# Expert choice: wider table rows from kept buffers, scales copied by ScalarE, and a new order of rows, statistics and choosing passes

## The chip, the core and the metric

The kernel runs on one core of a Trainium2 chip. Its engines work side by side, each through its own queue of instructions in order: TensorE (PE in the profile; PEld is its loading of weights), VectorE (DVE), ScalarE (ACT), GpSimd (POOL), and SyncE (SP), which here only issues DMA transfers. They wait for each other by semaphores. The metric is the device time of one execution in microseconds, the median of several runs.

## What is computed

The program is a four-layer network on an image tensor of 4 images, 128 channels and 64x64 positions. Each layer adds a convolution-like block and then a block on the tokens (the 4096 positions of an image, 128 values each) to the running tensor. The change concerns the token block of layers 1 and 2, a mixture of 64 experts in which each expert chooses its 8 best tokens of each image. Cut to what matters:

```python
def expert_choice(x, gate_w, gate_b, weight1, weight2):      # x: normed tokens, (4, 4096, 128)
    logits = einsum('bsd,ed->bse', x, gate_w) + gate_b       # 64 experts
    probs = softmax(logits, axis=1)                          # over the tokens of an image
    topv, topi = top_k over tokens, K = 8                    # per image and expert
    gathered = x[b, topi]                                    # (4, 8, 64, 128)
    pooled = einsum('bked,bke->bed', gathered, topv)
    h = gelu(einsum('ebd,edh->ebh', [pooled, 1], weight1))   # 512 hidden values
    out = einsum('ebh,eho->ebo', [h, 1], weight2)
    outputs[b, topi] += out * topv
    return outputs

t = t + expert_choice(layernorm(t), ...)                     # in layers 1 and 2
```

## The kernel before

The running tensor `xs` stays on chip for the whole program, channels on the 128 partitions and the 4096 tokens of each image along the free dimension. `net.chunk(b, c)` is a block of 512 tokens (`CH`) of image `b`; an image has 8 of them (`NCH`). The phases of the network run one after the other; `expert_choice(net, layer)` (L911) is called once in layer 1, after the deformable convolution, and once in layer 2, after a 3x3 convolution. Inside it all engines execute instructions in the order in which the Python code issues them (`tc.manual_schedule`), so the loops at the end of a stage are a schedule written out by hand. A tile pool hands out buffers; `bufs=5` means that the sixth tile of this tag waits until the first is no longer used. `bank("a", ...)` and `bank("b", ...)` are PSUM banks, three of each.

The work is done for pairs of images: pair 0 is images 0 and 1, pair 1 is images 2 and 3. A pair fills the partitions as 2 images x 64 experts, so the logits of a pair, `chosen[p]`, are 128x4096.

**Stage 1, choosing** (pool `moe_a`). At the start SyncE loads the gate, the biases and the weights of the first 3 of 16 groups of experts (L985, L987).
- `stat(p, j)` (L1008, L1010): TensorE centres a block, ScalarE squares it; every fourth block `variances` (L1018) sums squares over channels by four small products. 16 blocks for a pair.
- `scales(p)` and `inverted(p)` (L1031, L1035): square root on ScalarE and reciprocal on VectorE give 1/standard deviation of each token, as rows; `turn_scales(p)` (L1041, L1043) transposes them, so that a token's scale stands in its partition.
- `logits(p, c)`: TensorE spreads the scales over the partitions with a column of the identity, one product for each image (L1054), and multiplies the gate with the tokens (L1062). ScalarE copies the spread scales out of PSUM (L1066), VectorE multiplies (L1067), ScalarE adds the bias (L1068).
- `largest(p)`: VectorE finds the 8 largest of 4096 (L1087), their places (L1090), and the row numbers; two passes over 128x4096.
- `exponentials(p, neg)`: ScalarE takes the exponential of all logits, with their sum (L1101), and of the 8 (L1103). One buffer, `exps`, serves both pairs.
- `rows(b, c)`: the tokens are written to a table in DRAM, one row for each token. TensorE transposes four times 128 tokens (L1076), ScalarE copies them to `moe_xt` (L1078), GpSimd puts the token's scale behind the 128 values (L1079), and SyncE writes the block of 512 rows (L1081). A row has `ROW` = 129 numbers, 516 bytes. 8 blocks for an image, 32 in a call.
- `ask(p, j)` (L1108): GpSimd gathers, for each expert and image of the pair, the row of its j-th choice, by an indirect DMA.
- `pool(p)`: VectorE makes diagonal matrices of share x scale (L1122), TensorE sums the gathered rows with them (L1130), ScalarE copies (L1132), TensorE centres (L1134), VectorE puts the result into `pooled` (L1135).
- `mark(p)` (L972) and `choose(p)` (L977): VectorE overwrites the 8 largest logits with a mark, and then turns the whole 128x4096 into exponentials where the mark is and zero elsewhere. They are needed only in stage 3.

The order of stage 1 before: two statistics, the gate product (L1142) and the transposes of the first bias (L1147), the other statistics of pair 0, five of pair 1, the logits of pair 0, `largest(0)`, the rest of pair 1's statistics, the exponentials of pair 0, then the rows of images 0 and 1 with the logits of pair 1 between, then the rows of images 2 and 3 with the last logits, `largest(1)`, `mark(0)`, `choose(0)` and the gathers of pair 0; the exponentials and gathers of pair 1; `pool(0)`, `pool(1)`.

**Stage 2, experts** (pools `moe_b`, `moe_w_b`). 16 groups of 4 experts. `first` (L1201) and `second` (L1227) are the two products, `turn` (L1213, L1215, L1220) transposes, adds the bias and applies the gelu, `hand` (L1246) collects the results. Each group's weights are 2 MB. Five buffers hold them: three taken at the start of the call, two in memory that stage 1 used, so that SyncE's fourth load waits for the end of stage 1. VectorE also does `mark(1)` in turn 4 and `choose(1)` in turn 7 of the loop.

**Stage 3** (L1278, L1282): one product per block brings the experts' results back to the chosen tokens, and VectorE adds it to `xs`.

Of the kernel before, what the change touches and what calls it, by code (L numbers as in the profile page):

```python
# [910 lines left out]
def expert_choice(net, layer):  # L911
# [19 lines left out]
    PAIRS = B // 2  # L931
    K, ROW = 8, P + 1
    EARLY, LATE = 3, 2
    GONE = -3.0e38
    w1, w2 = ins[f"L{layer}_ffn_weight1"], ins[f"L{layer}_ffn_weight2"]
    with ExitStack() as ctx:
# [30 lines left out]

        tops = {}

        def mark(p):  # L970
# [20 lines left out]
        with (  # L991
# [56 lines left out]
            def logits(p, c):  # L1048
                pb, pl = bank("b", "rb"), bank("a", "pl")
                q = c % 4  # L1050
                rows = slice(32 * q, 32 * q + 32)
                for i in range(2):
                    own = 32 * q + 2 * i + c // 4
                    nc.tensor.matmul(  # L1054
                        pb[i * E : (i + 1) * E],
                        net.ident[rows, own : own + 1].to_broadcast([32, E]),
                        rstds[p][rows],
                        start=True,
                        stop=True,
                    )  # L1060
                for i in range(2):
                    nc.tensor.matmul(  # L1062
                        pl[i * E : (i + 1) * E], cgate, net.chunk(2 * p + i, c), start=True, stop=True
                    )
                lg = chosen[p][:, c * CH : (c + 1) * CH]
                nc.scalar.copy(lg, pb)  # L1066
                nc.vector.tensor_mul(lg, lg, pl)  # L1067
                nc.scalar.activation(lg, lg, AF.Identity, bias=gbias)  # L1068

            def rows(b, c):  # L1070

                p, i = divmod(b, 2)
                pt = bank("b", "pt")
                for t in range(4):
                    tok = slice((4 * c + t) * P, (4 * c + t + 1) * P)
                    nc.tensor.transpose(pt[:, t * P : (t + 1) * P], net.xs[:, b, tok], net.ident)  # L1076
                xt = sb.tile([P, 4, ROW], F32, name="moe_xt", tag="moe_xt", bufs=5)
                nc.scalar.copy(xt[:, :, 0:P], pt.rearrange("p (t d) -> p t d", d=P))  # L1078
                nc.gpsimd.tensor_copy(xt[:, :, P], turned[p][:, i, c, :])  # L1079
                first = i * N + c * CH  # L1080
                nc.sync.dma_start(tables[p][first : first + CH, :].rearrange("(t p) r -> p t r", p=P), xt)  # L1081
# [3 lines left out]
            def largest(p):  # L1085
# [9 lines left out]
                nc.vector.tensor_copy(places[p], row)  # L1095
                neg = sb.tile([P, 1], F32, name="moe_neg", tag="moe_neg")
                nc.vector.tensor_scalar_mul(neg, top[:, 0:1], -1.0)
                return neg

            def exponentials(p, neg):  # L1100
                nc.scalar.activation(exps, chosen[p], AF.Exp, bias=neg, accum_out=totals[p])  # L1101
                shares[p] = sb.tile([P, K], F32, name="moe_share", tag="moe_share")
                nc.scalar.activation(shares[p], tops[p], AF.Exp, bias=neg)  # L1103

# [33 lines left out]

            for j in range(2):
                stat(0, j)  # L1140
            pg = bank("b", "pg")
            nc.tensor.matmul(pg[:, 0:E], net.cent, gate, start=True, stop=True)  # L1142
            nc.vector.tensor_copy(cgate, pg[:, 0:E])

            pg = bank("b", "pb").rearrange("p (i c) -> p i c", i=NH)
            for i in range(NH):
                nc.tensor.transpose(pg[:, i, 0:E], b1[:, i:HID:NH], net.ident[0:E, 0:E])  # L1147
            nc.vector.tensor_copy(b1t, pg[:, :, 0:E])
            for j in range(2, 2 * NCH):
                stat(0, j)  # L1150
            scales(0)
            inverted(0)
            for j in range(5):
                stat(1, j)
            turn_scales(0)
            for c in range(NCH):
                logits(0, c)
            neg = largest(0)
            for j in range(5, 2 * NCH):
                stat(1, j)  # L1160
            scales(1)
            exponentials(0, neg)
            inverted(1)
            for n in range(2 * NCH):
                rows(*divmod(n, NCH))
                if n == 5:
                    turn_scales(1)
                if n > 5 and n % 2 == 0:
                    logits(1, n // 2 - 3)
            for n in range(2 * NCH):  # L1170
                rows(2 + n // NCH, n % NCH)
                if n < 6 and n % 2 == 0:
                    logits(1, 5 + n // 2)
                if n == 5:
                    neg = largest(1)
                    mark(0)
                    choose(0)
                if 5 < n < 6 + K:
                    ask(0, n - 6)
            exponentials(1, neg)  # L1180
            for j in range(K):
                ask(1, j)
            pool(0)
            pool(1)

        ob = ctx.enter_context(tc.tile_pool(name="moe_out", bufs=1))
        ots = [ob.tile([P, D], F32, name=f"moe_ot{i}") for i in range(PAIRS)]
        with (
# [66 lines left out]
            for g in range(GROUPS + 3):  # L1255
# [6 lines left out]
                if 0 <= g - 3:  # L1262
                    hand(g - 3, outs.pop(g - 3))
                if g == 4:
                    mark(1)
                if g == 7:
                    choose(1)
# [705 lines left out]
```

## Time and profile before

| what | us |
|---|---|
| median of 3 runs | 8528.07 (8521.14 to 8533.63) |
| the profiled execution, its own time | 8199.67 |
| span of the profiled execution, first to last instruction | 8197.9 |
| layer 1, stage 1 (from 2795.9) | 141.3 |
| layer 1, stage 2 (from 2937.2) | 80.1 |
| layer 1, stage 3 (from 3017.3) | 20.4 |
| layer 2, stage 1 (from 3356.9) | 137.0 |
| layer 2, stage 2 (from 3493.9) | 81.6 |
| layer 2, stage 3 (from 3575.5) | 20.5 |

Busy shares of the whole span on the profile's page: TensorE 92%, VectorE 67%, GpSimd 65%, ScalarE 46%. In stage 1 of layer 1 (141.3 us) the windows view gives busy times of 109.3 (TensorE), 53.0 (VectorE), 68.4 (ScalarE) and 26.5 (GpSimd), and a mean DMA share of 0.56.

How to read the lines below. A line of a timeline gives start and length in us, the engine, the line of the kernel, the operation, the tile written and the tiles read, the shape and the number of instructions merged; the bracket is the idle time of the engine before it and what ended it. "SPq" is SyncE issuing a DMA. A window line gives the length and the busy times of the engines in it with their instruction counts. The mean clock that TensorE was granted was 0.965 of full.

### The profile page before, as it was taken

What the parts mean: (1) busy time and instruction counts of PE and PEld (TensorE: products, weight loads), DVE (VectorE), ACT (ScalarE), POOL (GpSimd) and SP (SyncE); (2) the same over time, 40 slices, a digit from 0 to 9 for tenths busy, and PEclk for the clock granted to TensorE, in tenths of its full rate; (3) what the DMA queues carried; (4) which work ended last, traced back from release to release, by engine and by line L of the source; (5) the groups of instructions that cost most, each with busy time, mean ns of one, the idle gap of its engine ahead of it and who ended that gap; (6) DMA issues with size and microseconds to landing.
All of it is one profiled execution on the core that took longest, in us unless ns stands there. A gap on an engine that the chain in (4) does not pass through costs nothing.

```text
span 8197.9 us, 144876 instructions
## 1 busy us (share of the span) xinstructions
PE 7560.4 (92%) x59022; PEld 3232.8 (39%) x59022; DVE 5530.6 (67%) x8689; ACT 3768.7 (46%) x7100; POOL 5299.3 (65%) x3019
## 2 busy tenths in 40 slices
PE   8999986777777779879999999999999999999899
PEld 2222243555555434333444344443444434444333
DVE  6888856888888642247776667766677677677155
ACT  4444433444444420313555555555555555555521
POOL 5888904777777410104888788887788777888700
PEclk9999998999999989988999999999999999999999
DMA  6434206877877570232554445554545444455400
GB/s 183 93 77 95 50 2 158 249 220 237 241 217 209 161 211 0 46 146 57 108 110 105 103 105 104 110 106 99 107 101 111 105 101 106 106 105 110 98 22 24
DMA packets 333940, 963.78 MB, mean 118 GB/s; under 512 B 43412, under 2 KB 148948, under 8 KB 275412
## 3 DMA queue, kind: packets, MB, share of 16 engines
q0 software_dynamic: 143872, 673.30, 34.9%
q1 hardware_dynamic: 189396, 281.18, 12.7%
q8 instruction: 464, 7.60, 0.4%
q14 instruction: 208, 1.70, 0.1%
HBM read 468.89 MB, written 82.78 MB: 67 GB/s over the span
## 4 chain that ended last, share of the span: by engine, by line
PE 53%; DVE 2%; issue 1%; DMA 1%; ACT 0%; POOL 0%; SPq 0%; POOLq 0%; DVEq 0%; ACTq 0%
PE att_pv L1576 15%; PE att_sc L1663 13%; PE att_mx L1520 11%; PE att_sc L1564 5%; PE top_po L1876 3%; PE top_pw L1852 1%; DVE att_most L1531 1%; DMA moe_w<-in_L_ffn_weight 1%; PE att_sc L1493 0%; PE att_sc L1607 0%; PE att_sc L1624 0%; PE top_po L1874 0%; PE att_mx L1418 0%; PE att_sc L1454 0%; PE att_sc L1520 0%
## 5 line engine op out<-in xcount | busy, mean ns | idle before, releaser
L1595 POOL TENSOR_TENSOR att_acc<-att_acc,att_ex 128x2048 f32<-128x2048 f32 x640 | 2902.3, 4535 | 637.5 <-ACT att_ex L1664 618.1
L1531 DVE TENSOR_REDUCE att_most<-att_mx 128x2 f32<-128x1024 f32 x2016 | 2461.9, 1222 | 1071.3 <-PE att_mx L1520 992.7
L1664 ACT ACTIVATE att_ex<-att_sc 128x512 f32<-128x512 f32 x4096 | 2223.7, 594 | 1771.1 <-PE att_sc L1663 1488.0
L1663 PE MATMUL att_sc<-att_q,att_k 32*128 32x512 f32 x8192 | 2455.6, 606 | 0.0
L1520 PE MATMUL att_mx<-att_k,att_q 32*128 32x512 f32 x8064 | 2292.1, 647 | 12.9 <-DVE att_parts L1543 10.8
L1564 PE MATMUL att_sc<-att_rows,att_ones_b 32*128 32x256 bf16 (+1 forms) x6144 | 1502.5, 306 | 4.7 <-ACT att_ex L1664 4.7
L816 POOL DMA_INDIRECT dcn_g<-dcn_table,dcn_idx x1152 | 1100.8, 956 | 433.4 <-DMA dcn_g<-dcn_table,dcn_idx 122.5
L1576 PE MATMUL att_pv<-att_ex,att_vals 128*32 128x256 f32 x16384 | 1309.8, 391 | 0.0
L1520 PEld LDWEIGHTS att_mx<-att_k,att_q 32*128 32x128 f32 x8064 | 610.9, 185 | 867.1 <-issue 707.2
L409 POOL TENSOR_TENSOR inv_prod<-inv_seen,inv_prod 128x512 f32<-128x512 f32 (+1 forms) x672 | 837.4, 1273 | 95.4 <-ACT inv_prod L408 95.4
L411 DVE SCALAR_TENSOR_TENSOR inv_prod<-inv_pk,bspan,inv_seen 128x512 f32<-128x512 f32 (+1 forms) x1120 | 774.5, 743 | 141.4 <-PE inv_pk L398 141.1
L1576 PEld LDWEIGHTS att_pv<-att_ex,att_vals 128*32 128x32 f32 x16384 | 322.5, 108 | 1318.9 <-issue 1300.8
L1663 PEld LDWEIGHTS att_sc<-att_q,att_k 32*128 32x128 f32 x8192 | 818.3, 183 | 11.0 <-issue 8.3
L830 ACT ACTIVATE dcn_one<-dcn_g,dcn_w 128x128 f32<-128x128 f32 x1152 | 458.0, 401 | 790.9 <-DMA dcn_g<-dcn_table,dcn_idx 785.6
L857 PE MATMUL dcn_pt<-ident,dcn_sum 128*128 128x128 f32 x2304 | 513.3, 306 | 248.9 <-DVE dcn_sum L841 247.8
L408 ACT ACTIVATE inv_prod<-inv_pk,bspan 128x512 f32<-128x512 f32 (+1 forms) x672 | 436.7, 683 | 504.3 <-PE inv_pk L398 493.2
L856 PE MATMUL dcn_pt<-ident,dcn_one 128*128 128x128 f32 x2304 | 481.2, 292 | 93.3 <-ACT dcn_st L873 81.3
L398 PE MATMUL inv_pk<-inv_red,wtap 32*96 32x512 f32 (+1 forms) x3584 | 512.0, 637 | 7.2 <-DVE wtap L376 7.2
L856 PEld LDWEIGHTS dcn_pt<-ident,dcn_one 128*128 128x128 f32 x2304 | 395.2, 202 | 304.7 <-issue 140.2
L857 PEld LDWEIGHTS dcn_pt<-ident,dcn_sum 128*128 128x128 f32 x2304 | 368.4, 201 | 329.3 <-DVE dcn_sum L841 328.5
L833 DVE TENSOR_SCALAR dcn_part<-dcn_g,dcn_w 128x128 f32<-128x128 f32 x1152 | 405.5, 352 | 124.5 <-DMA dcn_g<-dcn_table,dcn_idx 92.3
L420 PE MATMUL inv_out<-inv_prod,inv_fold 96*32 96x512 f32 (+1 forms) x3584 | 478.5, 606 | 8.5 <-DVE xs L428 8.5
(346 smaller groups left out, 6878.9 us busy)
## 6 DMA issues: line engine op xcount, KB each, us to landing
att_sum<-att_ex POOLq DMA_DIRECT2D x320, 1024.0 KB, 7.4
inv_seen<-inv_image SPq DMA_DIRECT2D x256, 266.0 KB
moe_w<-in_L_ffn_weight SPq DMA_DIRECT2D x64, 1024.0 KB
dcn_table<-dcn_xt SPq DMA_DIRECT2D x64, 512.0 KB
att_sum<-att_ex SPq DMA_DIRECT2D x32, 1024.0 KB
att_sum<-att_acc POOLq DMA_DIRECT2D x32, 1024.0 KB, 7.7
dcn_g<-dcn_table,dcn_idx POOLq DMA_INDIRECT x1152, 3.8
moe_table<-moe_xt SPq DMA_DIRECT2D x64, 258.0 KB
```

The costliest lines, as they stand in the source:

```text
L409: nc.gpsimd.tensor_mul(of, view, of)
L411: nc.vector.scalar_tensor_tensor(out=of, in0=as_shape(pk[0:m], of), scalar=by, in1=view, op0=ALU.add, op1=ALU.mult)
L816: nc.gpsimd.indirect_dma_start(out=g, out_offset=None, in_=rows, in_offset=bass.IndirectOffsetOnAxis(ap=idx[:, j + i, k : k + 1], axis=0),)
L856: nc.tensor.matmul(out, one_, net.ident, start=i == 0, stop=False)
L857: nc.tensor.matmul(out, s, net.ident, start=False, stop=i == 3)
L1520: nc.tensor.matmul(pm[i] if alone else pm[:, i, :], q[r, t * P : (t + 1) * P], ks[r, kc * CH : (kc + 1) * CH], start=True, stop=True,)
L1531: nc.vector.tensor_reduce(most[:, 2 * half : 2 * half + 2, kc], pm, AX.X, ALU.max)
L1564: nc.tensor.matmul(pe[:, cols], ones_b[r], lows[g][r, cols], start=cols.start == 0, stop=False)
L1576: nc.tensor.matmul(block["pv"][r, cols], vals[b][:, t, r], ex[:, h, cols], start=t == 0 and half == 0, stop=t == NT - 1 and half == 1,)
L1595: nc.gpsimd.tensor_add(block["acc"], block["acc"], ex)
L1663: nc.tensor.matmul(pe, ks[r, t * P : (t + 1) * P], qs[c][r], start=False, stop=True)
L1664: nc.scalar.activation(ex[:, h, :], pe, AF.Exp)
```

## The change

All of it is in `expert_choice`.
- A row of the table has 144 numbers (576 bytes) instead of 129; the 15 added ones are zeros that GpSimd writes once at the start. The five buffers of `rows` are kept by name and used in turn.
- The token's scale is copied into the row by ScalarE instead of GpSimd.
- In `logits`, one product with a prepared selector `own` (made by 16 GpSimd copies at the start) spreads the scales of both images.
- The gate product stands behind `turn_scales(0)`, the bias transposes between `pool(0)` and `pool(1)`.
- The first four row blocks stand between the second statistics of pair 1. `largest(1)` comes behind all logits, with two row blocks between two logits.
- The exponential of pair 1 in stage 1 is taken in eight pieces into scratch, for its sum alone; the full one, into `exps`, is taken in turn 5 of the experts.
- `mark(0)` and `choose(0)` move to turns 2 and 4 of the experts, `choose(1)` from turn 7 to 9, `mark(1)` from 4 to 7.

```diff
--- before.py
+++ after.py
@@ -929,7 +929,7 @@
     GROUPS = E // EG
     CG = P // EG
     PAIRS = B // 2
-    K, ROW = 8, P + 1
+    K, ROW = 8, P + 16
     EARLY, LATE = 3, 2
     GONE = -3.0e38
     w1, w2 = ins[f"L{layer}_ffn_weight1"], ins[f"L{layer}_ffn_weight2"]
@@ -966,6 +966,7 @@
         nc.gpsimd.memset(behind[E:P], float(N))
 
         tops = {}
+        negs = [keep.tile([P, 1], F32, name=f"moe_neg{p}") for p in range(PAIRS)]
 
         def mark(p):
             lg = chosen[p]
@@ -1049,15 +1050,7 @@
                 pb, pl = bank("b", "rb"), bank("a", "pl")
                 q = c % 4
                 rows = slice(32 * q, 32 * q + 32)
-                for i in range(2):
-                    own = 32 * q + 2 * i + c // 4
-                    nc.tensor.matmul(
-                        pb[i * E : (i + 1) * E],
-                        net.ident[rows, own : own + 1].to_broadcast([32, E]),
-                        rstds[p][rows],
-                        start=True,
-                        stop=True,
-                    )
+                nc.tensor.matmul(pb, own[rows, c // 4, :], rstds[p][rows], start=True, stop=True)
                 for i in range(2):
                     nc.tensor.matmul(
                         pl[i * E : (i + 1) * E], cgate, net.chunk(2 * p + i, c), start=True, stop=True
@@ -1067,6 +1060,20 @@
                 nc.vector.tensor_mul(lg, lg, pl)
                 nc.scalar.activation(lg, lg, AF.Identity, bias=gbias)
 
+            xts = [sb.tile([P, 4, ROW], F32, name=f"moe_xt{i}", bufs=1) for i in range(5)]
+            for t in xts:
+                nc.gpsimd.memset(t[:, :, P:ROW], 0.0)
+
+            own = sb.tile([P, 2, 2 * E], F32, name="moe_own", bufs=1)
+            for q in range(4):
+                group = slice(32 * q, 32 * q + 32)
+                for r in range(2):
+                    for i in range(2):
+                        at = 32 * q + 2 * i + r
+                        nc.gpsimd.tensor_copy(
+                            own[group, r, i * E : (i + 1) * E], net.ident[group, at : at + 1].to_broadcast([32, E])
+                        )
+
             def rows(b, c):
 
                 p, i = divmod(b, 2)
@@ -1074,9 +1081,9 @@
                 for t in range(4):
                     tok = slice((4 * c + t) * P, (4 * c + t + 1) * P)
                     nc.tensor.transpose(pt[:, t * P : (t + 1) * P], net.xs[:, b, tok], net.ident)
-                xt = sb.tile([P, 4, ROW], F32, name="moe_xt", tag="moe_xt", bufs=5)
+                xt = xts[(b * NCH + c) % len(xts)]
                 nc.scalar.copy(xt[:, :, 0:P], pt.rearrange("p (t d) -> p t d", d=P))
-                nc.gpsimd.tensor_copy(xt[:, :, P], turned[p][:, i, c, :])
+                nc.scalar.copy(xt[:, :, P], turned[p][:, i, c, :])
                 first = i * N + c * CH
                 nc.sync.dma_start(tables[p][first : first + CH, :].rearrange("(t p) r -> p t r", p=P), xt)
 
@@ -1093,14 +1100,21 @@
                 nc.vector.tensor_scalar(row, row, behind, None, op0=ALU.add)
                 places[p] = sb.tile([P, K], I32, name="moe_idx", tag="moe_idx")
                 nc.vector.tensor_copy(places[p], row)
-                neg = sb.tile([P, 1], F32, name="moe_neg", tag="moe_neg")
-                nc.vector.tensor_scalar_mul(neg, top[:, 0:1], -1.0)
-                return neg
-
-            def exponentials(p, neg):
-                nc.scalar.activation(exps, chosen[p], AF.Exp, bias=neg, accum_out=totals[p])
+                nc.vector.tensor_scalar_mul(negs[p], top[:, 0:1], -1.0)
+
+            def exponentials(p):
+
+                if p == 0:
+                    nc.scalar.activation(exps, chosen[p], AF.Exp, bias=negs[p], accum_out=totals[p])
+                else:
+                    sums = sb.tile([P, NCH], F32, name="moe_sums", bufs=1)
+                    for c in range(NCH):
+                        sq = sb.tile([P, CH], F32, name="moe_sq", tag="moe_sq", bufs=5)
+                        lg = chosen[p][:, c * CH : (c + 1) * CH]
+                        nc.scalar.activation(sq, lg, AF.Exp, bias=negs[p], accum_out=sums[:, c : c + 1])
+                    nc.vector.tensor_reduce(totals[p], sums, AX.X, ALU.add)
                 shares[p] = sb.tile([P, K], F32, name="moe_share", tag="moe_share")
-                nc.scalar.activation(shares[p], tops[p], AF.Exp, bias=neg)
+                nc.scalar.activation(shares[p], tops[p], AF.Exp, bias=negs[p])
 
             def ask(p, j):
                 if j == 0:
@@ -1136,51 +1150,46 @@
                     pooled[:, :, 2 * p : 2 * p + 2], pc.rearrange("p (i e) -> p e i", e=E)
                 )
 
-            for j in range(2):
-                stat(0, j)
-            pg = bank("b", "pg")
-            nc.tensor.matmul(pg[:, 0:E], net.cent, gate, start=True, stop=True)
-            nc.vector.tensor_copy(cgate, pg[:, 0:E])
-
-            pg = bank("b", "pb").rearrange("p (i c) -> p i c", i=NH)
-            for i in range(NH):
-                nc.tensor.transpose(pg[:, i, 0:E], b1[:, i:HID:NH], net.ident[0:E, 0:E])
-            nc.vector.tensor_copy(b1t, pg[:, :, 0:E])
-            for j in range(2, 2 * NCH):
+            for j in range(2 * NCH):
                 stat(0, j)
             scales(0)
             inverted(0)
             for j in range(5):
                 stat(1, j)
             turn_scales(0)
+            pg = bank("b", "pg")
+            nc.tensor.matmul(pg[:, 0:E], net.cent, gate, start=True, stop=True)
+            nc.vector.tensor_copy(cgate, pg[:, 0:E])
             for c in range(NCH):
                 logits(0, c)
-            neg = largest(0)
+            largest(0)
             for j in range(5, 2 * NCH):
                 stat(1, j)
+                if j % 3 == 0:
+                    rows(0, j // 3 - 2)
             scales(1)
-            exponentials(0, neg)
+            exponentials(0)
             inverted(1)
-            for n in range(2 * NCH):
-                rows(*divmod(n, NCH))
-                if n == 5:
-                    turn_scales(1)
-                if n > 5 and n % 2 == 0:
-                    logits(1, n // 2 - 3)
-            for n in range(2 * NCH):
-                rows(2 + n // NCH, n % NCH)
-                if n < 6 and n % 2 == 0:
-                    logits(1, 5 + n // 2)
-                if n == 5:
-                    neg = largest(1)
-                    mark(0)
-                    choose(0)
-                if 5 < n < 6 + K:
-                    ask(0, n - 6)
-            exponentials(1, neg)
+            for c in range(4, NCH):
+                rows(0, c)
+            turn_scales(1)
+            for c in range(NCH):
+                logits(1, c)
+                for n in (2 * c, 2 * c + 1):
+                    rows(1 + n // NCH, n % NCH)
+            largest(1)
+            for c in range(NCH):
+                rows(3, c)
+                ask(0, c)
+            exponentials(1)
             for j in range(K):
                 ask(1, j)
             pool(0)
+
+            pg = bank("b", "pb").rearrange("p (i c) -> p i c", i=NH)
+            for i in range(NH):
+                nc.tensor.transpose(pg[:, i, 0:E], b1[:, i:HID:NH], net.ident[0:E, 0:E])
+            nc.vector.tensor_copy(b1t, pg[:, :, 0:E])
             pool(1)
 
         ob = ctx.enter_context(tc.tile_pool(name="moe_out", bufs=1))
@@ -1261,9 +1270,15 @@
                     outs[g - 2] = second(g - 2, act.pop(g - 2), t2.pop(g - 2))
                 if 0 <= g - 3:
                     hand(g - 3, outs.pop(g - 3))
+                if g == 2:
+                    mark(0)
                 if g == 4:
+                    choose(0)
+                if g == 5:
+                    nc.scalar.activation(exps, chosen[1], AF.Exp, bias=negs[1])
+                if g == 7:
                     mark(1)
-                if g == 7:
+                if g == 9:
                     choose(1)
             for p in range(PAIRS):
                 nc.vector.tensor_add(ots[p], handed[:, p, :], b2)
```

## The prediction, made before the changed kernel ran

> **What bounds the kernel now.** I read the busy shares, then the chain of waits, then the timelines of each engine over the two stretches that the change touches. TensorE is busy for 92% of the 8197.9 us span, but that is an average over stages: the change lies only in the two calls of expert_choice, 2796 to 3038 us (layer 1) and 3357 to 3596 us (layer 2), together 481 us or 5.9% of the span. Each call has three stages: choosing and gathering (2795.9 to 2937.5; 3356.9 to 3494.2), 16 groups of experts (to 3017.3; to 3575), and adding to the residual.
>
> The start. In the timeline of TensorE for layer 1 the bracket is idle time and what ended it:
>
> ```profile
> 2800.89 0.41 PE L1142 MATMUL moe_pg<-moe_gate,cent 128*128 128x64 f32 x2 [3.02 <-DMA moe_gate<-in_L_ffn_gate_w]
> 2802.41 0.74 PE L1147 MATMUL moe_pb<-ident,moe_b 64*128 64x64 f32 x4 [1.12 <-DMA moe_b<-in_L_ffn_weight]
> 2803.09 6.44 PE L1008 MATMUL moe_pd<-xs,cent 128*128 128x512 f32 x8
> ...
> 2810.45 3.70 PE L1008 MATMUL moe_pd<-xs,cent 128*128 128x512 f32 x8
> ```
>
> TensorE waits twice for small loads, and the four statistics products behind the waits take 6.44 us where the next four take 3.70: it restarts at a lower clock.
>
> The logits. ScalarE and VectorE hand one block of 512 tokens to and fro:
>
> ```profile
> 2831.96 0.56 ACT L1066 COPY moe_chosen<-moe_rb 128x512 f32<-128x512 f32 x1
> 2833.35 0.72 ACT L1068 ACTIVATE moe_chosen<-moe_chosen,moe_gbias 128x512 f32<-128x512 f32 x1 [0.82 <-DVE moe_chosen L1067]
> 2833.97 0.57 ACT L1066 COPY moe_chosen<-moe_rb 128x512 f32<-128x512 f32 x1
> ```
>
> One block takes 2.01 us (2831.96 to 2833.97), and ScalarE waits only for VectorE. TensorE needs about the same, 1.0 us for L1054 and 1.0 us for L1062.
>
> The rows. The timelines of SyncE's queue, GpSimd, VectorE and ScalarE, layer 1:
>
> ```profile
> 2866.10 52.18 SPq L1081 DMA_DIRECT2D moe_table<-moe_xt  x32
> ```
>
> ```profile
> 2912.88 4.59 POOL L1079 COPY moe_xt<-moe_turned 128x4 f32<-128x4 f32 x2
> 2923.47 0.97 POOL L1108 DMA_INDIRECT moe_asked<-moe_table,moe_idx  x1 [6.00 <-DVE moe_share L1118]
> ...
> 2932.23 0.94 POOL L1108 DMA_INDIRECT moe_asked<-moe_table,moe_idx  x1 [0.30 <-issue]
> ```
>
> ```profile
> 2912.87 4.42 DVE L977 SCALAR_TENSOR_TENSOR moe_chosen<-moe_chosen,moe_exp 128x4096 f32<-128x4096 f32 x1
> ```
>
> Thirty-two writes to the tables leave in 52.18 us. The last two four-column copies on GpSimd take 4.59 us instead of 0.19 each, exactly while VectorE's L977 pass runs. Only when the last row has landed can the eight gathers of the second table start (2923.47); they are issued 1.25 us apart, and all later work stands behind them.
>
> The experts. The windows view (length, then busy time of PE, PEld, DVE, ACT, POOL, clock, DMA share, GB/s) and the chain of waits in layer 2:
>
> ```profile
> 2937.20:3017.30 80.10, 61.83 (x770) 33.56 (x770) 19.26 (x44) 14.57 (x33) 0.00 (x0) 0.87 0.94 343
> ```
>
> ```profile
> 3502.26 14.28 DMA moe_w<-in_L_ffn_weight
> ```
>
> This stage is the weight stream: 13 groups of 2 MB arrive every 5.4 us, VectorE and ScalarE are busy for 24% and 18% of it.
>
> [...]
>
> **The change part by part.** Times are from the first statistics product of a call; pairs are layer 1 / layer 2, read from the timelines.
>
> *Gate and bias transposes off the start.* The statistics of the first pair end at 27.5 / 24.4 us now. Without waits they are four rounds of four products and their variances, 4.63 us each (2810.45 to 2815.08): 18.5 us. That is 9.0 / 5.9 us less, of which 4.1 / 2.7 us are the waits and the rest is clock and the moved products. The gate product comes back behind the scales (0.41 us, its load long landed), so the logits start at 23.9 instead of 32.5 / 29.3 us. The bias transposes (0.74 us) go between the two pools, beside gathers in flight. If the clock stayed low the gain would be the waits alone; that is the lower end.
>
> *One selecting product for two.* L1054's pair (1.0 us) becomes one product over 128 columns, some 0.5 us. In the first logits the 2.01 us loop of ScalarE and VectorE stays, so I count only 0.5 us once, at the loop's start: largest(0) ends at 51 us. The 16 small GpSimd copies that make the selector, at 0.19 us like L1079's, take 3 us from the call's start and are needed at 23.9: nothing.
>
> *First four row blocks beside the second statistics.* TensorE gets 4 x 0.54 us of transposes more there, ScalarE 4 x 0.8 us, in 15 us where it is busy for 7.4. Those statistics ended at 63.6 / 60.3; now they end at about 55 (41 plus some 14). Square root, table load and the 3.71 us exponential follow as before, so ScalarE is free for rows at 61 instead of 69.6 / 66.3, and four of 32 blocks are already written.
>
> *Scales copied by ScalarE.* 32 copies of 128x4 more. The nearest row is the 128x8 activation L1103, 0.28 us, whose successor starts after 0.19; I take 0.2 (0.1 to 0.28). In the second logits a block with two rows now needs on ScalarE 2.01 + 2 x (0.5 + 0.2) = 3.4 us, where layer 2 ran at 3.04 us, bound by TensorE, and layer 1 near 3.5 with waits for rows. TensorE falls to 2.6. Eight blocks from 64 end at 91 us. The last logits are there at 90.3 us instead of 102.8 / 98.7, the indices at 100.
>
> *Rows of 576 bytes.* Layer 2 writes two blocks each 3.04 us without ScalarE waiting for a landing: 1.52 us per block, 174 GB/s. The 512 byte rows of the deformable table are written at 178 GB/s with a DMA share of 0.98, so the cost is mostly per row. I take 1.52 again; bounds: 1.45 if aligned rows are easier, 1.70 if it goes by bytes (1.52 x 576/516). From 62 us, 27 further blocks x 1.52, eight gathers of the first table x 0.37 (1.89 us per block with a gather beside it, less 1.52) and 4.6 us from last issue to gather (3475.1 to 3479.7 in layer 2) give 62 + 41 + 3 + 4.6 = 110.5 us for the second table's first gather, against 127.6 / 122.8. The GpSimd stall goes with the copies: GpSimd's queue holds only gathers now, and the first table's wait for nothing but its landing.
>
> *Behind the last row.* The second exponential is eight pieces: 8 x (0.6 + 0.19) = 6.3 us instead of 3.9. It ends near 111, and pool(0), queued behind its sum on VectorE, by 117. The eight gathers run from 110.5 to 120.5, so pool(1) still ends with them, 14.0 us after the first (2923.47 to 2937.50). There are 3.5 us of cover; if it is gone, pool(0) is late next.
>
> *Four passes and one exponential among the experts.* Added per call: L972 and L977 for the first pair (8.8 us of VectorE), a 3.71 us exponential and two table loads of 1.28. Behind a pass wait the bias addition and the output copy of a group, then TensorE's second product, then the freeing of its weight buffer. Before, two such passes ran here, and the weights kept arriving each 5.4 us, with TensorE waiting only for DMA (16.1 us). Each pass fits into one group's time. I count nothing; bound: 0 to 4.4 us per call.
>
> **The sum.** Layer 1: 127.6 - 110.5 = 17.1 us. Layer 2: 122.8 - 110.5 = 12.3 us. Together 29.4, say 30, with a little for the ends: 8199.67 becomes about 8170 us. The profiled execution is 328 us shorter than the median of the runs, 8528.07. I take the 30 us off that as they are (31 if all stretches by 4%): 8498 us.
>
> **The rivals.** *Rows and ScalarE cost more.* At 1.70 us a block 27 x 0.18 = 4.9 us per call are given back, at 0.28 us a copy another 2.5, 15 in all: 8513 us. For it: half of what is left of the wait is this stream. Against: layer 2's pace. 0.2. *Aligned rows are cheaper and the slack larger*, 1.40 us a block: 6.5 more, with the ends some 40 us in all: 8488 us. 0.1. *The expert stage becomes the bound on the other side.* If the weight queue has no slack behind VectorE, the four passes (17.7), the exponential and its loads (6.3) add 24 us per call, 48 in two: 8528 - 30 + 48 = 8546 us. It decides from 15 us per call on. For it: VectorE and ScalarE run in order and hold a group's buffers. Against: two passes cost nothing before. 0.07.
>
> **How the numbers follow.** My forecast, gain 22 to 38 us (8490 to 8506), has 0.63. This kernel's runs differ by 0.15%, so 0.2%, 17 us, is about what can be told from no change. The forecast, the cheaper rows and half of the dearer ones lie above: faster 0.82. Half of the dearer rows and small losses elsewhere: within 0.11; the expert stage: slower 0.07. The range, 8484 to 8518, takes the forecast, the cheaper rows and most of the dearer.
>
> **What would show it.** No idle before the statistics and 18.5 us for the first pair; first logits still 2.01 us a block; SyncE's 32 row writes starting near 43 us; no GpSimd copy in the rows; second table's first gather near 110 us; experts still some 80 us with weights each 5.4. It is wrong if row writes leave more than 1.7 us apart, if the experts exceed 84 us, or if TensorE waits for VectorE there.

## The result: 29 us faster, and the profile after

| | before | after |
|---|---|---|
| median of the runs, us | 8528.07 (7 runs, 8520.07 to 8535.39) | 8498.65 (7 runs, 8487.47 to 8507.32) |
| ratio after / before, 95% interval | | 0.9964 [0.9954, 0.9974] |
| profiled execution: span, mean granted TensorE clock | 8197.9, 0.965 | 8500.6, 0.933 |
| layer 1: stage 1 / experts, us | 141.6 / 79.8 | 122.6 / 81.3 |
| layer 2: stage 1 / experts, us | 137.3 / 81.3 | 126.2 / 79.9 |

The interval is 22 to 39 us. The two profiles cannot be subtracted as wholes: they were taken at different granted clocks, and the call of layer 1 begins at 2795.9 us in one and at 3122.3 in the other, behind code that is the same in both. All comparisons below are therefore made within a stage, from the first statistics product of a call to the last write of `pooled` (stage 1) and from there to the first product of stage 3 (experts); the table ahead puts that border 0.3 us earlier, so it has 141.3 and 137.0. In the changed kernel the lines of `expert_choice` carry other numbers; they are named as they come.

The start, in the timeline of TensorE of the kernel after, layer 1:

```profile
3122.29 5.42 PE L1009 MATMUL moe_pd<-xs,cent 128*128 128x512 f32 x12 [0.84 <-DVE xs L883]
...
3139.80 1.80 PE L1019 MATMUL moe_pv<-moe_sq,ewin 128*32 128x512 f32 x8
...
3146.77 1.12 PE L1053 MATMUL moe_rb<-moe_rstd,moe_own 32*128 32x512 f32 x2
3147.82 1.08 PE L1055 MATMUL moe_pl<-xs,moe_cgate 128*64 128x512 f32 x4
```

Six products, two instructions each, run without a gap in 5.42 us; both waits for loads are gone, and so is the low clock behind them: the granted clock is 1.00 in these 5.42 us, and it was 0.57 in the 6.44 us behind the waits of before (2803.09 to 2809.53). The last variance of pair 0 ends 19.3 us after the start (3141.60 - 3122.29), the logits begin at 24.5. The one selecting product, L1053, takes 1.05 us (3146.77 to 3147.82). In the timeline of before the same job is the pair of half products:

```profile
2830.43 1.07 PE L1054 MATMUL moe_rb<-moe_rstd,ident 32*64 32x512 f32 x4
2831.43 1.08 PE L1062 MATMUL moe_pl<-xs,moe_cgate 128*64 128x512 f32 x4
```

Four records of 0.61 us each on average lie in 1.07 us, so the two halves already ran side by side: a pair took 1.00 us (2830.43 to 2831.43). One product in place of two, at 1.05 us, saved nothing.

The rows and the second logits, in the timelines of SyncE's queue and of TensorE, layer 1:

```profile
3167.72 59.07 SPq L1088 DMA_DIRECT2D moe_table<-moe_xt  x32
```

```profile
3186.09 0.90 PE L1083 MATMUL moe_pt<-ident,xs 128*128 128x128 f32 x4 [5.09 <-ACT moe_xt L1085]
3186.79 1.06 PE L1042 MATMUL moe_pr<-ident,moe_rstd 128*128 128x128 f32 x4
3187.78 2.07 PE L1053 MATMUL moe_rb<-moe_rstd,moe_own 32*128 32x512 f32 x2
3189.78 1.98 PE L1055 MATMUL moe_pl<-xs,moe_cgate 128*64 128x512 f32 x4
...
3205.76 1.12 PE L1053 MATMUL moe_rb<-moe_rstd,moe_own 32*128 32x512 f32 x2
3206.81 1.08 PE L1055 MATMUL moe_pl<-xs,moe_cgate 128*64 128x512 f32 x4
3207.82 1.09 PE L1083 MATMUL moe_pt<-ident,xs 128*128 128x128 f32 x8
3208.85 1.12 PE L1053 MATMUL moe_rb<-moe_rstd,moe_own 32*128 32x512 f32 x2
```

The first write leaves at 45.4 us, and the last is issued by 104.5. TensorE stands still for 5.09 us while ScalarE takes pair 0's exponential and cannot empty the transposes. Then one block of the second logits (two in layer 2) runs at half speed: L1053 2.07 us instead of 1.12. The windows view has a granted clock of 0.50 from 3186.79 to 3192 us and of 1.00 from 3198 to 3204. A full speed block is 3.09 us (3205.76 to 3208.85) with no gap in it: 1.05 + 1.01 + 1.03 is TensorE's own work.

The second table's first gather, in GpSimd's timeline, and the experts of layer 1, in the windows and in the waits of TensorE (total us, times, longest):

```profile
3230.73 0.94 POOL L1122 DMA_INDIRECT moe_asked<-moe_table,moe_idx  x1 [12.76 <-DMA moe_table<-moe_xt]
```

```profile
3244.85:3326.10 81.25, 61.65 (x768) 34.16 (x768) 27.35 (x47) 20.73 (x36) 0.00 (x0) 0.87 0.93 339
```

```profile
PE moe_ph L1210 <- DMA moe_w<-in_L_ffn_weight: 17.8, 12, 2.6
```

The gather starts 108.4 us after the first statistics product (112.0 in layer 2; 127.6 and 122.8 before), and still waits for the last rows. The experts hold 8.4 us more of VectorE's work than before, counted from the same border, and are still the weight stream: of TensorE's waits there 17.8 us are for weights and 1.2 for all else.

### The profile page after: what moved, and what is told of

Same layout as the page of the kernel before. It is cut to its first block, busy times and chain, and to the rows that moved or that the text cites. A ratio compares the mean times of both kernels' runs of the same rounds, so it can differ in the third digit from the quotient of the medians.

```text
span 8500.6 us, 144747 instructions
## 1 busy us (share of the span) xinstructions
PE 7633.4 (90%) x58958; PEld 3314.4 (39%) x58958; DVE 5537.3 (65%) x8691; ACT 3701.0 (44%) x7198; POOL 5286.2 (62%) x2997
## 4 chain that ended last, share of the span: by engine, by line
PE 51%; DVE 2%; issue 1%; DMA 1%; ACT 0%; POOL 0%; SPq 0%; POOLq 0%; ACTq 0%; DVEq 0%
PE att_pv L1591 15%; PE att_sc L1678 13%; PE att_mx L1535 10%; PE att_sc L1579 5%; PE top_po L1891 3%; PE top_pw L1867 1%; DVE att_most L1546 1%; DMA moe_w<-in_L_ffn_weight 1%; PE att_sc L1508 0%; PE att_sc L1639 0%; PE att_sc L1622 0%; PE top_po L1889 0%; PE att_mx L1433 0%; PE att_sc L1469 0%; PE att_sc L1535 0%
## 5 line engine op out<-in xcount | busy, mean ns | idle before, releaser
L856 PE MATMUL dcn_pt<-ident,dcn_one 128*128 128x128 f32 x2304 | 527.2, 314 | 235.5 <-ACT dcn_st L873 112.5
L856 PEld LDWEIGHTS dcn_pt<-ident,dcn_one 128*128 128x128 f32 x2304 | 444.5, 225 | 474.0 <-issue 300.6
L873 ACT COPY dcn_st<-dcn_pt 128x512 f32<-128x512 f32 x288 | 166.3, 577 | 909.9 <-remote 530.1
L857 PEld LDWEIGHTS dcn_pt<-ident,dcn_sum 128*128 128x128 f32 x2304 | 418.3, 224 | 183.1 <-issue 119.3
L841 DVE SCALAR_TENSOR_TENSOR dcn_sum<-dcn_g,dcn_w,dcn_part 128x128 f32<-128x128 f32 x1152 | 352.2, 345 | 201.6 <-remote 111.3
```

The source lines that it names most:

```text
L856: nc.tensor.matmul(out, one_, net.ident, start=i == 0, stop=False)
L857: nc.tensor.matmul(out, s, net.ident, start=False, stop=i == 3)
```

## The experiments

Stage 1 repeats well except for one thing: in how many blocks of the second logits TensorE runs at half clock (L1053 at 2.07 us, not 1.12). So two lengths are given for each run: as measured, and less the half clock, which is the time from the first to the eighth selecting product of the second logits, less seven blocks of 3.09 us (3.04 with half products). The changed kernel has 122.6 and 126.2 us, of which 2.5 and 5.2 are half clock: 120.1 and 121.0 net. The runs came from three chips, whose whole times for the kernel before differ (8540.8, 8195.7 and 8196.0 us); only stages are compared between them. Each run has one trace, and a difference of 2 us between two traces is not yet a finding (see the next part).

| run | stage 1, layer 1 / 2 | half clock in it | net, against the changed kernel |
|---|---|---|---|
| e1_start | 136.9 / 129.6 | 8.1 / 2.7 | +8.7 / +5.9 |
| e2_early | 121.7 / 122.6 | 0 / 0 | +1.6 / +1.6 |
| e3_passes | 129.2 / 128.9 | 5.2 / 5.4 | +3.9 / +2.5 |
| e4_gpsimd | 122.9 / 124.4 | 3.0 / 2.2 | -0.2 / +1.2 |
| e7_both | 131.6 / 125.7 | 7.9 / 2.4 | +3.6 / +2.3 |
| e5_row516 | 128.9 / 131.2 | 2.9 / 5.1 | +5.9 / +5.1 |
| e10_row544 | 124.5 / 125.9 | 5.2 / 5.2 | -0.8 / -0.3 |
| e11_row528 | 124.6 / 126.7 | 2.9 / 5.3 | +1.6 / +0.4 |
| e8_lateexp | 116.0 / 118.2 | 0 / 1.6 | -4.1 / -4.4 |
| e9_late_halves | 116.6 / 115.2 | 1.6 / 0 | -5.1 / -5.8 |

### The kernel before, profiled again

> The kernel before, unchanged, profiled a second time. If stage lengths repeat from one execution to the next, its first stages take 141.6 and 137.3 us again within 1 us (experts 79.8 and 81.3 within 2), although the span of its first profile, 8197.9 us, was 330 us below the median of its runs. If the first stage itself varies by several us, differences of that size between two traces prove nothing.

139.2 and 136.6 us, experts 79.8 and 80.0, at a granted clock of 0.933 and a span of 8535.9. Layer 1 differs by 2.4 us from its first profile, layer 2 by 0.7: the stage lengths hardly follow the mean clock of the execution. The 2.4 us are more than the 1 us expected, so 2 us is about what one trace can tell. The 330 us between the first profile and the median go with that clock and lie almost wholly outside the changed code.

### The start undone

```diff
-            for j in range(2 * NCH):
-                stat(0, j)
+            for j in range(2):
+                stat(0, j)
+            pg = bank("b", "pg")
+            nc.tensor.matmul(pg[:, 0:E], net.cent, gate, start=True, stop=True)
...
+                nc.tensor.transpose(pg[:, i, 0:E], b1[:, i:HID:NH], net.ident[0:E, 0:E])
+            nc.vector.tensor_copy(b1t, pg[:, :, 0:E])
+            for j in range(2, 2 * NCH):
+                stat(0, j)
```

Both pieces are taken out of their new places.

> The changed kernel with the gate product and the bias transposes back behind the first two statistics products. First stage of the changed kernel: 122.6 and 126.2 us. My theory, that the start lies on the chain to the second table's last row: pair 0's statistics end at 27.5 and 24.4 us again instead of 19.3, and the first stage becomes 8 and 5 us longer (130.8 and 131.3). Rival, that the row stream sets the end and the start has slack: at most 2 us longer.

The statistics of pair 0 end at 27.0 and 24.6 us again, stage 1 is 14.3 and 3.4 us longer, net 8.7 and 5.9. The rival, slack at the start, is out: the statistics end 7.7 and 5.3 us later than in the changed kernel, and the stage is longer by about as much. The raw numbers miss the expectation only through the half clock, three blocks in one layer and one in the other. The run also bears out that half clock is to be taken off as it is: layer 1 has 5.4 us more of it than layer 2 and statistics that end 2.5 us later, and its stage 1 is 7.3 us longer.

### The early rows undone

```diff
-                if j % 3 == 0:
-                    rows(0, j // 3 - 2)
...
-            for c in range(4, NCH):
+            for c in range(NCH):
                 rows(0, c)
```

> The changed kernel with the first four row blocks no longer beside the second statistics but behind them, in front of the other four. My theory, that the rows are a stream at about 1.5 us a block which ends last: four blocks more after 63 us, first stage 3 to 6 us longer (126 to 129 and 129 to 132). Rival, that the second logits and their indices end last, which have 5 us of slack to make up at most: under 1 us.

Not 3 to 6 us longer: 0.8 and 3.6 us shorter. All 32 writes now leave between 62.6 and 104.2 us, some 1.3 us a block, and end no later than in the changed kernel. That was the first sign that a row costs less than I had it. Net the early rows are worth 1.6 us, less than one trace can tell, and more than that is lost in clock in both layers. TensorE's timeline of this run, layer 1:

```profile
3202.34 3.73 PE L1083 MATMUL moe_pt<-ident,xs 128*128 128x128 f32 x20 [5.09 <-ACT moe_xt L1085]
3205.91 0.60 PE L1042 MATMUL moe_pr<-ident,moe_rstd 128*128 128x128 f32 x4
3206.44 1.12 PE L1053 MATMUL moe_rb<-moe_rstd,moe_own 32*128 32x512 f32 x2
```

The gap of 5.09 us is the same, but five blocks of transposes follow it (20 instructions). The slow time falls on them, 3.73 us for the 20 where twelve just ahead of the gap take 1.53 (3195.72), and the first selecting product is at full speed, 1.12 us. In the changed kernel one block of transposes follows, and the logits take the rest.

### The passes of pair 0 back in stage 1

```diff
-                if p == 0:
+                if True:
...
             largest(1)
+            mark(0)
+            choose(0)
...
-                if g == 2:
-                    mark(0)
                 if g == 4:
-                    choose(0)
-                if g == 5:
-                    nc.scalar.activation(exps, chosen[1], AF.Exp, bias=negs[1])
-                if g == 7:
                     mark(1)
-                if g == 9:
+                if g == 7:
                     choose(1)
```

The first two lines put the second exponential back into one piece, so none is left among the experts.

> The changed kernel with the match_replace and the is_equal pass of pair 0 back in the first stage, right behind the second indices, and with the second exponential in one piece (0 passes more among the experts than before). My theory: without GpSimd copies for them to stall, the passes (8.8 us, ending near 112 us) lie under the second table's gathers, and the first stage is 0 to 2 us longer; the expert stage keeps its 80 to 81 us. Rival A, that taking the passes out is what gave the gain: 5 to 9 us longer. Rival B, that they cost something among the experts: the expert stage becomes 2 us or more shorter.

Net 3.9 and 2.5 us longer, between my theory and rival A. GpSimd's and VectorE's timelines of this run show why; the two instructions lie side by side:

```profile
3245.37 4.31 POOL L1122 DMA_INDIRECT moe_asked<-moe_table,moe_idx  x1 [13.17 <-DMA moe_table<-moe_xt]
3249.98 0.94 POOL L1122 DMA_INDIRECT moe_asked<-moe_table,moe_idx  x1 [0.30 <-issue]
```

```profile
3244.43 4.42 DVE L978 SCALAR_TENSOR_TENSOR moe_chosen<-moe_chosen,moe_exp 128x4096 f32<-128x4096 f32 x1
```

The first gather of the second table takes 4.31 us instead of 0.94 and ends just behind the pass (3249.68 against 3248.85). The 3.4 us that it loses are about the net loss of layer 1. I had thought that only GpSimd's copies could be stalled; here a gather is, beside a pass that reads two inputs of 128x4096, both in SBUF. Beside the pass ahead of it, match_replace, which reads one such input, nothing was stalled in the kernel before: from 2908.41 to 2912.84 its copies took 0.19 us each and its gathers 0.97. Why GpSimd is slow beside the one and not beside the other is not shown. Rival B is out: the experts take 79.8 and 79.9 us with fewer passes, against 81.3 and 79.9 with them, and 79.7 to 81.7 over all runs.

### The scales copied by GpSimd, alone and with the passes

```diff
-                nc.scalar.copy(xt[:, :, P], turned[p][:, i, c, :])
+                nc.gpsimd.tensor_copy(xt[:, :, P], turned[p][:, i, c, :])
```

> The changed kernel with GpSimd copying the scales into the rows again, while pair 0's passes stay among the experts. My theory, that the copies as such cost GpSimd 0.19 us and that only a two-input pass of VectorE stalls them: first stage 0 to 3 us longer than in the changed kernel (up to 3 because a copy now stands behind a gather of the first table that waits for its landing). Rival, that ScalarE's copies are what sped the rows up: 5 us longer or more.

> The changed kernel with both undone: GpSimd copies the scales, and match_replace and is_equal of pair 0 run behind the second indices. e3_passes alone cost 2.7 us in layer 2, where a gather took 4.31 us instead of 0.94 during the is_equal pass. My theory: the pass now stalls row copies too, so the second table's first gather comes 4 us later than with either part alone, and the first stage is 6 to 10 us longer than in the changed kernel. Rival, that the two are independent: the sum of their single costs, 3 to 5 us.

(The 4.31 us named there belong to layer 1.) Alone: -0.2 and +1.2 us net. ScalarE's copies are not what sped the rows up. With the passes: 3.6 and 2.3, no more than the passes alone. My expectation of 6 to 10 was wrong: the rows now leave so early that the last copy (2902.14 us) is made before the is_equal pass begins (some 4.4 us later, behind match_replace), so only the gather is stalled (layer 1, 5.13 us). In the kernel before, the last two copies fell into that pass (4.59 us); the stall was theirs only because the rows were late.

### Rows of 516, 528 and 544 bytes

```diff
-    K, ROW = 8, P + 16
+    K, ROW = 8, P + 1
```

The same with `P + 4` and `P + 8` for 528 and 544 bytes.

> The changed kernel with rows of 129 values, 516 bytes. With the early rows undone (e2_early) 32 blocks of 576 byte rows left in 41.6 us, 1.34 us a block; the forecast had 1.52 for both sizes. Theory A, that rows of 576 bytes really are cheaper: the write stream of 516 bytes runs at 1.5 us or more where nothing else holds it, and the last table write and the second table's first gather come 2 to 5 us later. Theory B, that 1.52 was the pace of TensorE or GpSimd and not of the writes: no difference beyond 1 us once the first selecting products run at the same clock.

> The changed kernel with rows of 132 values, 528 bytes, a multiple of 16 and not of 32. If 16 is enough: first gather of the second table 14 to 16 us after the last logits; if it takes 32: about 20 us, as with 516. If the cost grew smoothly with alignment, in between.

> The changed kernel with rows of 136 values, 544 bytes, a multiple of 32 and not of 64. 516 byte rows left at 189 GB/s with the stream saturated, 576 byte rows faster. If a multiple of 32 is enough: behind the second logits the stream runs at 250 GB/s or more and the second table's first gather comes 14 to 16 us after the last logits, as with 576. If it takes 64, or if the size of the row counts: about 20 us after the last logits, as with 516.

Theory A holds: the first gather comes 20.5 and 21.1 us after the last logits with 516 bytes, 16.3 and 16.5 with 528, 13.7 and 15.5 with 544 (14.7 and 15.9 with 576). Where ScalarE waits for writes to land, in the run with 516 bytes, layer 1, it copies a block of rows every 1.59 us (six intervals, 2887.85 to 2897.41):

```profile
2887.85 0.59 ACT L1085 COPY moe_xt<-moe_pt 128x512 f32<-128x512 f32 x1 [1.70 <-DMA moe_table<-moe_xt]
...
2895.76 0.59 ACT L1085 COPY moe_xt<-moe_pt 128x512 f32<-128x512 f32 x1 [1.30 <-DMA moe_table<-moe_xt]
2897.41 0.59 ACT L1085 COPY moe_xt<-moe_pt 128x512 f32<-128x512 f32 x1 [0.97 <-DMA moe_table<-moe_xt]
```

The windows view of such stretches, where the DMA share is above 1 (columns as in the prediction; the last is GB/s), for 516, 528 and 544 bytes, and for 576 in e8_lateexp below:

```profile
2887.00:2898.50 11.50, 4.00 (x16) 2.56 (x16) 7.01 (x7) 5.19 (x15) 0.94 (x1) 0.60 1.20 189
```

```profile
2888.70:2898.20 9.50, 2.68 (x18) 1.68 (x16) 7.38 (x7) 4.97 (x17) 0.37 (x1) 0.82 1.17 246
```

```profile
2889.90:2897.40 7.50, 3.27 (x22) 2.09 (x20) 7.43 (x4) 4.78 (x16) 0.27 (x1) 0.89 1.12 280
```

```profile
2883.00:2890.00 7.00, 3.09 (x20) 1.90 (x19) 6.96 (x3) 4.47 (x13) 0.08 (x1) 1.00 1.11 308
```

SyncE's queue (q1) in the DMA view of the same four stretches, with packets, MB and share:

```profile
q1 hardware_dynamic: 3925, 1.96, 112.8%
```

```profile
q1 hardware_dynamic: 4258, 2.18, 109.6%
```

```profile
q1 hardware_dynamic: 3766, 1.99, 104.7%
```

```profile
q1 hardware_dynamic: 3711, 2.08, 106.0%
```

Counted as 512 packets, one for each of its rows, a block takes 1.50, 1.14, 1.02 and 0.97 us; counted by the MB, 1.55, 1.18, 1.05 and 0.99. (ScalarE's 1.59 us follow the landings of five blocks earlier, one turn of the buffers, and are not the pace of the full stream. The other bytes in the windows are gathers of the first table.) The wider row is the cheaper one, although it carries more bytes. Of the 0.53 us that 576 bytes save, 544 bytes save 0.48 and 528 bytes 0.36; in stage 1, net, 544 bytes lose nothing against 576 (-0.8 and -0.3 us) and 528 bytes little (1.6 and 0.4), where 516 lose 5.9 and 5.1. Whether the starts of the rows or their lengths decide was not separated: both change together here. Nor is every row of a round length cheap: the deformable table of this program has rows of 512 bytes, and at the 178 GB/s that the prediction names, 512 of them take 1.47 us. Those writes differ in more than the row (they come from 64 partitions and go to every fourth row place), and no run here tells why they are slow.

### The first exponential behind the rows

```diff
             scales(1)
-            exponentials(0)
             inverted(1)
...
                 rows(3, c)
                 ask(0, c)
+            exponentials(0)
             exponentials(1)
             for j in range(K):
                 ask(1, j)
             pool(0)
+            total(1)
```

`total(1)` is VectorE's sum of the eight pieces, taken out of `exponentials(1)`.

> The changed kernel with the first pair's exponential (table load and 3.71 us) behind the last rows instead of in front of the second logits, and the sum of the second one's pieces behind the first pool. Theory: in the changed kernel TensorE stands idle for 5.09 us behind that exponential and then runs one to three blocks of the second logits at half clock; the loop itself, 3.11 us a block, is TensorE's own work. Without the gap the second logits end at 87 to 89 us in both layers, with no selecting product of 2.07 us, and the first stage takes 114 to 118 us (5 to 10 shorter). Rival, that 11 us of exponentials in a row then end last behind the gathers: 121 us or more.

TensorE's timeline of this run, layer 1:

```profile
2854.85 0.66 PE L1042 MATMUL moe_pr<-ident,moe_rstd 128*128 128x128 f32 x4 [2.25 <-DVE moe_rstd L1036]
2855.43 1.12 PE L1053 MATMUL moe_rb<-moe_rstd,moe_own 32*128 32x512 f32 x2
```

The gap shrinks from 5.09 to 2.25 us, and the first selecting product runs at full speed, 1.12 us. The second logits end at 87.7 and 88.8 us (93.7 and 96.1 in the changed kernel), stage 1 is 6.6 and 8.0 us shorter. In layer 2 the gap is 2.25 us as well, and 1.6 us of half clock remain; they begin only behind the first selecting product. The exponentials fit under the gathers: the rival is out.

### The same with half products, timed

```diff
-                nc.tensor.matmul(pb, own[rows, c // 4, :], rstds[p][rows], start=True, stop=True)
+                for i in range(2):
+                    half = slice(i * E, (i + 1) * E)
+                    nc.tensor.matmul(pb[half], own[rows, c // 4, half], rstds[p][rows], start=True, stop=True)
```

> e8_lateexp with the selecting product again as two products of 64 columns, timed against the kernel before. The pair of half products took 1.0 us before the change and the single product of 128 columns 1.05. My theory: one product for two saves nothing, and where a loop is TensorE's own work the halves save 0.05 us a block, 16 blocks, so the first stage is 0.5 to 1 us shorter than e8_lateexp's 116.0 and 118.2. Rival, my forecast's step, that a single product takes half the time: the halves cost 0.5 us a block in the second logits, 4 us. Against the kernel before, by the first stages of its second profile (139.2 and 136.6) less 115 and 117: 43 us less, a ratio of 0.9950 +- 0.0010; the changed kernel had 0.9964.

A block of the second logits takes 3.04 us against 3.09: two half products are a little cheaper than one, not dearer. Over 16 blocks that is 0.8 us; stage 1 is net 1.0 and 1.4 us shorter than in e8_lateexp, which one trace alone could not tell. Five runs: 8156.29 us against 8196.01 for the kernel before (9 runs), ratio 0.9953 [0.9940, 0.9967], 40 us, where 43 were expected. In stage 1 this version is 6.0 and 11.0 us shorter than the changed kernel; the two were not timed against each other, and their intervals overlap.

## Why the prediction was right, and where it was not

8498 was forecast, 8498.65 measured; with an interval of 17 us, so close a hit is luck. The first gather of the second table was forecast at 110.5 us and came at 108.4 and 112.0. But the sum is right partly because errors in its terms cancel, and that is luck too. Point by point:

- **The start.** Right. 9.0 and 5.9 us forecast, 8.7 and 5.9 net by undoing it. The statistics end at 19.3, not 18.5.
- **One selecting product for two.** Wrong. "Becomes one product over 128 columns, some 0.5 us": it takes 1.05. I divided the pair's time by two without asking whether the two halves ran one after the other. From this came also "TensorE falls to 2.6": it stays at 3.09 and sets the second loop, not ScalarE with the 3.4 us that I had.
- **The early rows.** Wrong. I counted four blocks of 1.52 us as gone from the stream behind ScalarE. They are worth 1.6 us net at most, and the version without them is no slower.
- **Scales by ScalarE.** 0.2 us each as forecast, and half of it overlaps its neighbours. The step away from GpSimd is worth 0 to 1.2 us.
- **Rows of 576 bytes.** The term that was most wrong: 1.52 us a block, with 1.45 to 1.70 as bounds; 0.97 measured. I read 1.52 as the pace of the writes in a loop where no wait for a landing showed, but that loop of 3.04 us for two blocks was TensorE's own, as the prediction itself says under the scales. That rows of 516 bytes take 1.50 when the stream is full is a coincidence. That the cost is mostly per row, which kept the 1.52 for the wider rows, was my estimate: it came from 174 and 178 GB/s at 516 and 512 bytes, two sizes too close to show it. The 1.45, and the 1.40 of the rival, were guesses that no trace stood behind. The rival with cheaper rows had the direction. Its size was too small, 6.5 us for both calls against 5.9 and 5.1, 11 in all, and it came in place of other terms, not on top.
- **What I had not counted.** The half clock behind ScalarE's exponential, 2.5 and 5.2 us. A gap of 5.1 us was there before too, but four blocks of transposes lay behind it, ahead of the second logits; they took the slow time, as the five do in e2_early. TensorE's timeline of before, layer 1, where twelve transposes take 2.82 us at a granted clock of 0.50 that at 1.00 take 1.53 (2859.47, just ahead of the gap):

```profile
2859.47 1.53 PE L1076 MATMUL moe_pt<-ident,xs 128*128 128x128 f32 x12
2866.09 2.82 PE L1076 MATMUL moe_pt<-ident,xs 128*128 128x128 f32 x12 [5.09 <-ACT moe_xt L1078]
```

- **The passes.** Right among the experts: no cost that can be told. In stage 1, put back, they cost 3.9 and 2.5 us, in layer 1 through a stalled gather (4.31 us); in the kernel before it was two copies that stalled (4.59 us).
- **Behind the first gather.** 14.0 forecast, 14.1 and 14.2 measured. The eight pieces took 5.75 us instead of 6.3.

The parts add up, within the 2 us of a trace. Undone singly, net, they cost 8.7 + 1.6 + 3.9 - 0.2 + 5.9 = 19.9 us in layer 1 and 5.9 + 1.6 + 2.5 + 1.2 + 5.1 = 16.3 in layer 2. From the kernel before (139.2, 136.6) to the changed kernel net of the half clock (120.1, 121.0) it is 19.1 and 15.6; the slow transposes of the kernel before are not taken off. The half clock gives back 2.5 and 5.2; that leaves 27 us of stage 1 in two calls, inside the 22 to 39 of the runs. So the start has 14.6 us of the gain, the wider rows 11, the passes 6.4, the rest little. The new order of rows, second logits and `largest(1)` was not undone by itself.

Of the two larger rivals, the dearer rows fell with the 0.97 us, and the expert stage as a bound with its 79.7 to 81.7 us in every run. The rival's 24 us a call counted four passes, although two of them had stood there before; the added work was 15.

## What to carry to other kernels

Before a step is priced by a loop's pace, ask which engine sets that pace: a wait that does not show says nothing of a stream that was never full. Rows written to DRAM one by one can be worth padding: here 512 rows took 1.50 us at 516 bytes and 0.97 at 576. Before saving bytes, try a wider row, and measure it, since the 512 byte rows of the deformable table are slow all the same (1.47 us). And when work is moved, look at what then stands first behind an idle gap of TensorE: here it ran at a granted clock of 0.50 behind a gap of 5.09 us.

## What I had not expected of the hardware

- With the stream full, writing 512 rows from 128 partitions, counted as 512 packets, took 1.50 us at 516 bytes a row, 1.14 at 528, 1.02 at 544 and 0.97 at 576.
- A gather by GpSimd took 4.31 us instead of 0.94 while VectorE ran a pass of 4.42 us with two inputs in SBUF (e3_passes, layer 1).
- Behind a gap of 5.09 us TensorE stayed slow for up to three blocks of the second logits of 5.8 us each, 17 us of work without a gap in its timeline (e1_start, layer 1, 3221.74 to 3239.16: L1053 took 2.07 us three times, then 1.12). Why it varies between layers and runs stays open.
- One product of 128 columns took 1.05 us, two of 64 columns side by side 1.0 (32 rows, 512 columns of tokens, f32).
